# A second attention written out in a fixed order on three engines, with its PSUM banks in three groups

## The chip, the cores and the metric

The kernel runs on one core of one Trainium2 chip. The metric is the device time of one execution in microseconds (us). Before the change the median of 3 runs is 1372.56 us (1369.76 to 1373.3). One further execution was profiled, and everything said of single instructions comes from it.

## The reference, cut to what matters

A batch of 32 sequences of 128 tokens, each token 128 wide, goes through two layers. Each has an attention part and a feed-forward part, both with residual additions, all in fp32.

```python
x = x + L0_attn(L0_cond(x, cond))     # modulated linear layer, 16 heads of 64, causal
x = x + L0_ffn(L0_cond2(x, cond))     # gated recurrence, then three coupling cycles
x = x + L1_attn(L1_cond(x, cond))     # experts, then 16 heads of 8
x = x + L1_ffn(L1_cond2(x, cond))     # low-rank adapter, then a slot memory
```

The change lies in the second layer. Its parts are, shortened:

```python
def L1_cond(x, c):                    # 2 of 4 experts per sequence, and a shared one
    out = sum_e(w[b, e] * mask[e] * (gelu(x @ ew1[e] + eb1[e]) @ ew2[e] + eb2[e]))
    return out + gelu(x @ sw1 + sb1) @ sw2 + sb2

def L1_attn(x, Wq, bq, Wk, bk, Wv, bv, gamma, beta):      # H = 16, dh = 8
    Q, K, V = relu(x @ Wq + bq), relu(x @ Wk + bk), relu(x @ Wv + bv)
    scores = einsum('bqhd,bkhd->bhqk', Qh, Kh) / sqrt(dh)
    scores = where(key_mask == 0 or above the diagonal, NEG, scores)
    out = einsum('bhqk,bkhd->bqhd', softmax(scores) * query_mask, Vh)
    out = out + x
    return gamma * (out - mean(out)) / sqrt(var(out) + 1e-8) + beta

def L1_ffn(x):                        # 64 slots
    alpha = softmax over the 8 best of 64 of (gelu([x, mean(slots)] @ w1 + b1) @ w2 + b2)
    S = GRU(slots, alpha.T @ x / sum(alpha));  S = layernorm(S + selfattention(S))
    return (alpha @ (S @ wvp + bvp)) @ wo + bo
```

## The kernel before, in words

The activations stay in SBUF as `X`, transposed: 128 features on the partitions, 4096 tokens along the free axis. Work goes by chunks of 4 sequences (512 tokens, `CB`, `CH`), 8 chunks in all. The first layer takes the first half of the time and the second layer the rest.

Instructions are written in Python in program order; a scheduler of the framework then orders them on each engine by its own estimate of when their inputs are there, and gives each tile a buffer. Where a call goes through `keep_in_program_order`, the instruction may not be moved ahead of what was written just before it on its engine. Before the change only ACT's activations are held so (`act`, line 337). TensorE and DVE are free. Every PSUM tile is one bank (128 x 512 fp32) and comes from one pool of 8 (`ps`, line 264).

The second layer runs in 4 turns of 32 steps (loop from line 1247), two chunks a turn, here called a and c.

- Steps 0 to 23 are the experts, `experts` (788): per chunk four pieces for the shared expert and eight for the chosen ones. A chosen piece gathers its weights with an indirect DMA issued by POOL (`ew`), makes four hidden blocks on TensorE, four Gelu activations on ACT (`he`), four accumulating matmuls, and two DVE operations that add the result to `xm`.
- `attention_inputs` (827) makes queries, keys, values, mask and residual of a chunk, with six PSUM banks: for a at step 13, for c at step 24.
- Steps 24 to 31 are the attention. A unit is one sequence (`attention`, 865), eight units a turn. Its 16 heads are four groups of four; a group fills one PSUM bank. A unit takes five calls of `advance` (1229), so that five units are under way: `scores` (POOL makes the head-masked keys `km`; four mask matmuls and four score matmuls into four banks), `weights` (per group a DVE maximum, `s1max`, and four exponentials on ACT, `s`), `turned` (per group four transposes, then a copy to SBUF `p1T` on DVE or ACT), `values` (16 small matmuls, a copy `oS` on ACT) and `normed` (four transposes, the division by the sums on DVE, the residual addition on POOL, and the statistics `bn_stats`, `bn_aggr` on DVE).
- After the eighth unit one more `advance` stands in step 31, and three stand in steps 0, 1 and 2 of the next turn, after the expert piece of that step. They drain the last units.
- The rest of a turn's work is generators that take one step an iteration, set by `plan` (1207 to 1226): `after_attention` (953), `hidden`, `routes_top`, `routes` during the next turn's experts, `slots_new` (1057) from its steps 22 and 23, and `slots_told` (1113) from its steps 29 and 30, beside the next turn's attention. After the last turn they run alone.

ACT swaps its function table (`ACT_TABLE_LOAD`) between the Gelu of the experts and the exponential of the attention. `shared` (793) is the first piece of a turn: a matmul from `X`, a Gelu `hid`, a second matmul.

## Time and profile before

| what | value |
| --- | --- |
| median of 3 runs | 1372.56 us (1369.76 to 1373.3) |
| the profiled execution, its own time | 1377.57 us |
| its span, first to last instruction | 1375.8 us |
| mean granted TensorE clock in it | 0.932 |
| busy: TensorE, ACT, DVE, POOL | 1190.6, 782.6, 759.2, 495.4 us |
| weight loads of TensorE (beside the matmuls) | 721.4 us |
| maxima of the second attention on DVE (L888) | 128, first at 770.6, last at 1282.4 us |
| exponentials of the second attention on ACT (L339, `s`) | 512, mean 399 ns |

Busy time is an average over stages. What the change can move lies between 760 and 1300 us, where turns of experts and attention alternate; the first maxima of the four turns stand at 770.6, 913.0, 1070.6 and 1231.2 us. Idle time in front of an instruction is put down in the profile to what released it. "Granted clock" is the share of full speed that TensorE was given in a stretch. In a row of the timeline the instructions of one kind that follow each other are merged, and the time is from the first start to the last end; a row can begin before the one above it has ended, since matmuls overlap, so lengths are best taken from start to start.

### The profile page before, as it was taken

What the parts mean: (1) busy time and instruction counts of PE and PEld (TensorE: products, weight loads), DVE (VectorE), ACT (ScalarE), POOL (GpSimd) and SP (SyncE); (2) the same over time, 40 slices, a digit from 0 to 9 for tenths busy, and PEclk for the clock granted to TensorE, in tenths of its full rate; (3) what the DMA queues carried; (4) which work ended last, traced back from release to release, by engine and by line L of the source; (5) the groups of instructions that cost most, each with busy time, mean ns of one, the idle gap of its engine ahead of it and who ended that gap; (6) DMA issues with size and microseconds to landing.
All of it is one profiled execution on the core that took longest, in us unless ns stands there. A gap on an engine that the chain in (4) does not pass through costs nothing. (4 is left out here: it accounts for less than half of the span.)

```text
span 1375.8 us, 20779 instructions
## 1 busy us (share of the span) xinstructions
PE 1190.6 (87%) x7711; PEld 721.4 (52%) x7711; DVE 759.2 (55%) x1870; ACT 782.6 (57%) x2055; POOL 495.4 (36%) x444
## 2 busy tenths in 40 slices
PE   4999898979898998977787889898899989998865
PEld 1565554535554455534444556655567456665633
DVE  1445665565857558573433764466543665456744
ACT  2765565556657465642355774568545684658522
POOL 1655655465555555552544311221023110311100
PEclk9999999989999899978899999999999899999876
DMA  6000000000000000000242202320044001310000
GB/s 242 1 1 1 1 1 0 1 1 0 1 1 1 0 1 1 1 1 0 95 130 70 70 1 85 107 87 2 8 147 137 2 1 51 121 36 1 9 8 16
DMA packets 15988, 49.67 MB, mean 36 GB/s; under 512 B 1424, under 2 KB 5648, under 8 KB 15504
## 3 DMA queue, kind: packets, MB, share of 16 engines
q0 software_dynamic: 9504, 40.01, 9.3%
q1 hardware_dynamic: 5808, 7.29, 1.5%
q8 instruction: 61, 1.00, 0.3%
q10 hardware_dynamic: 576, 1.05, 0.2%
q14 instruction: 39, 0.32, 0.1%
HBM read 46.25 MB, written 2.10 MB: 35 GB/s over the span
## 5 line engine op out<-in xcount | busy, mean ns | idle before, releaser
L339 ACT ACTIVATE s_sb<-ps,s_max 128x128 f32<-128x128 f32 x512 | 139.0, 382 | 138.4 <-DVE s_max L426 134.8
L279 POOL TENSOR_TENSOR s_sb<-s_sb,s_sum 128x1024 f32<-128x1024 f32 x64 | 121.5, 1898 | 64.7 <-DVE s_sum L435 48.8
L339 ACT ACTIVATE s<-ps,s1max 128x128 f32<-128x128 f32 x512 | 138.1, 399 | 8.0 <-DVE s1max L888 8.0
L268 PE MATMUL ps<-hT,w_attn 128*128 128x512 f32 x256 | 126.2, 624 | 11.4 <-DVE hT L279 11.4
L279 POOL TENSOR_TENSOR s_half<-s_sb 128x512 f32<-128x512 f32 x64 | 82.5, 1289 | 117.1 <-ACT s_sb L339 116.9
L812 POOL DMA_INDIRECT ew<-in_expert,rows x64 | 62.6, 978 | 136.6 <-DVE ye L822 131.5
L339 ACT ACT_TABLE_LOAD x62 | 79.5, 1283 | 53.3 <-DVE s_max L426 38.9
L339 ACT ACTIVATE he<-ps,ew 128x128 f32<-128x128 f32 x256 | 72.6, 369 | 65.3 <-issue 31.2
L888 DVE TENSOR_REDUCE s1max<-ps 128x4 f32<-128x512 f32 x128 | 81.1, 682 | 50.5 <-PE ps L268 42.5
L339 ACT ACTIVATE qk<-ps 128x512 f32<-128x512 f32 x128 | 74.4, 615 | 59.6 <-PE ps L268 59.2
L426 DVE TENSOR_REDUCE s_max<-ps 128x4 f32<-128x512 f32 x128 | 81.0, 674 | 46.3 <-PE ps L268 46.2
L434 DVE TENSOR_REDUCE s_sum<-s_half 128x8 f32<-128x256 f32 x64 | 26.6, 416 | 132.6 <-POOL s_half L279 132.6
L268 PE MATMUL ps<-he,ew 128*128 128x128 f32 x512 | 82.2, 302 | 12.1 <-ACT he L339 11.2
L268 PEld LDWEIGHTS ps<-he,ew 128*128 128x128 f32 x512 | 72.3, 205 | 30.1 <-ACT he L339 27.4
L268 PEld LDWEIGHTS ps<-hT,w_attn 128*128 128x128 f32 x256 | 47.8, 196 | 69.7 <-issue 48.2
L279 POOL TENSOR_TENSOR km<-kT,w_base 128x512 f32<-128x512 f32 x32 | 34.4, 1074 | 132.9 <-PE ps L268 103.4
L268 PEld LDWEIGHTS ps<-qk 64*128 64x128 f32 x1024 | 65.1, 195 | 32.3 <-issue 32.3
L822 DVE SCALAR_TENSOR_TENSOR ye<-ps,ew 128x128 f32<-128x128 f32 x64 | 22.4, 350 | 105.6 <-PE ps L268 105.6
L898 PE MATMUL ps<-w_base,s 128*128 128x128 f32 x512 | 71.1, 287 | 9.8 <-DVE p1T L902 4.6
L268 PE MATMUL ps<-qk 64*128 64x128 f32 x1024 | 77.9, 294 | 0.0
L268 PE MATMUL ps<-pT,v 128*64 128x128 f32 x1024 | 72.4, 285 | 6.1 <-ACT pT L339 5.7
L444 PE MATMUL ps<-w_base,s_sb 128*128 128x128 f32 x512 | 73.9, 289 | 3.6 <-DVE oT L456 3.6
(300 smaller groups left out, 2480.2 us busy)
## 6 DMA issues: line engine op xcount, KB each, us to landing
w_attn<-in_attn POOLq DMA_DIRECT2D x2, 1024.0 KB, 10.5
out_x<-ot SPq DMA_DIRECT2D x8, 256.0 KB, 2.3
X<-in_xT ACTq DMA_DIRECT2D x4, 256.0 KB, 7.5
X<-in_xT SPq DMA_DIRECT2D x4, 256.0 KB, 9.3
w_lowr<-in_lowr SPq DMA_DIRECT2D x1, 1024.0 KB, 12.3
ew<-in_expert,rows POOLq DMA_INDIRECT x64, 4.5
w_ffn<-in_ffn SPq DMA_DIRECT2D x1, 928.0 KB, 10.2
w_mix<-in_mix SPq DMA_DIRECT2D x1, 800.0 KB, 11.1
```

The lines of the kernel that those rows point to most:

```text
L268: T.matmul(out_, lhsT=lhsT, rhs=rhs, start=start, stop=stop)
L279: eng.tensor_tensor(out_, a, b, op)
L339: return tc.keep_in_program_order(A.activation(*args, **kwargs))
L426: V.tensor_reduce(nm[:, 4 * par : 4 * par + 4], b3(two[par]), AX.X, ALU.max, negate=True)
L434: V.tensor_reduce(sm, half[:, :, 0:32], AX.X, ALU.add)
L444: T.transpose(p[:, bass.ts(i, S)], at["s"][:, 4 * par + i, :], ident)
L812: G.indirect_dma_start(ew, None, table, bass.IndirectOffsetOnAxis(ap=rows[:, r, k : k + 1], axis=0))
L822: V.scalar_tensor_tensor(t, y, ew[:, 1028:1029], ew[:, 1029:EW], ALU.add, ALU.mult)
L888: V.tensor_reduce(at["nm"][:, bass.ts(hg, 4)], b3(p), AX.X, ALU.max, negate=True)
L898: T.transpose(p[:, bass.ts(j, S)], at["s"][:, 4 * hg + j, :], ident)
```

## The change

Five things change, and no arithmetic is added or removed.

1. TensorE and DVE are wrapped so that, inside `advance`, each of their instructions is held in program order, as ACT's are already.
2. The one PSUM pool of 8 banks becomes three groups: A with 2, B with 3, C with 3. The first layer takes them in the turn A A B B B C C C. In the second layer every tile comes from C, with these exceptions: the experts' hidden blocks take B, their sums take A, and the attention's scores take the five of A and B in turn.
3. `attention` is cut into nine steps, and `advance` writes them out in one interleaving: the mask matmuls of the next unit are spread over the unit, one as each of the five banks comes free, and the copies out of PSUM are apart from what fills the bank.
4. The first unit's `advance` moves from step 24 to step 23, after the last expert piece, ahead of `attention_inputs` of chunk c. The other calls of `advance` move to the head of their iteration, ahead of its expert piece and generators.
5. `bn_stats` and `bn_aggr` move from `normed` to `after_attention`, and the `f_w1a` matmuls of both chunks are issued together for the odd one.

```diff
-    V, G, A, T = nc.vector, nc.gpsimd, nc.scalar, nc.tensor
+    pinned = []
+    class Pinned:
...
+            def call(*args, **kwargs):
+                ins = f(*args, **kwargs)
+                return tc.keep_in_program_order(ins) if pinned else ins
...
+    V, G, A, T = Pinned(nc.vector), nc.gpsimd, nc.scalar, Pinned(nc.tensor)
...
+    RING = "AABBBCCC"
+    turn = {"all": 0, "scores": 0}
+    short = []
+    def bank(tag):
+        return psum.tile([P, 512], F32, tag="ps" + tag, name="ps", bufs=RING.count(tag))
     def ps():
-        return psum.tile([P, 512], F32, tag="ps", name="ps")
+        if short:
+            return bank("C")
+        turn["all"] += 1
+        return bank(RING[(turn["all"] - 1) % 8])
+    def ps_scores():
+        turn["scores"] += 1
+        return bank(RING[(turn["scores"] - 1) % 5])
...
+        short.append(True)
...
             def shared(k):
-                p = ps()
+                p = bank("B")
...
-                    at["p"] = ps()
+                    at["p"] = bank("A")
...
-                    at["y"] = ps()
+                    at["y"] = bank("A")
...
-                p = ps()
+                p = bank("B")
...
+            def masks(hg):
+                if hg == 0:
+                    at["km"] = pool.tile([P, 4, S], F32, tag="km", name="km")
+                    tt(G, at["km"], outer(kT[:, cs], 4), inner(hmask, S), ALU.mult)
+                    at["p"] = []
+                p = ps_scores()
+                mm(p, ident16, outer(mask16[:, b], 4), stop=False)
+                at["p"].append(p)
...
-                st = pool.tile([P, 6], F32, tag="st", name="st", bufs=2)
-                V.bn_stats(st, Rb)
-                V.bn_aggr(MVs[g][:, b, :], st)
...
+            for b in range(CB):
+                st = pool.tile([P, 6], F32, tag="st", name="st", bufs=2)
+                V.bn_stats(st, R[:, b, :])
+                V.bn_aggr(mv[:, b, :], st)
...
-            if g % 2 == 0:
+            if g % 2:
                 HSs[g // 2] = ps()
-            e = slice(g % 2 * NS, g % 2 * NS + NS)
-            mm(HSs[g // 2][e], w("f_w1a"), xc)
+                for k in range(2):
+                    mm(HSs[g // 2][NS * k : NS * k + NS], w("f_w1a"), XCs[g - 1 + k])
...
-            for hg in range(4):
-                if w1:
-                    w1[1](hg)
-                if t1:
-                    t1[2](hg)
-            if v1:
-                v1[3]()
-            if item:
-                item[0]()
-            if n1:
-                n1[4]()
+            pinned.append(True)
+            do(item, "masks", 0)
+            do(w1, "highest", 0)
+            do(w1, "highest", 1)
+            do(t1, "turned", 0)
+            do(w1, "weights", 0)
+            do(t1, "kept", 0)
+            do(t1, "turned", 1)
+            do(t1, "turned", 2)
+            do(w1, "highest", 2)
+            do(t1, "kept", 1)
+            do(w1, "weights", 1)
+            do(t1, "kept", 2)
+            do(item, "masks", 1)
+            do(t1, "turned", 3)
+            do(w1, "highest", 3)
+            do(v1, "values")
+            do(item, "masks", 2)
+            do(w1, "weights", 2)
+            do(item, "masks", 3)
+            do(v1, "valued")
+            do(item, "scores")
+            do(w1, "weights", 3)
+            do(t1, "kept", 3)
+            do(n1, "normed")
+            pinned.pop()
...
+            if k < 3 and 1 <= r <= NP:
+                advance()
+            if k >= 24 and r < NP:
+                b = k - 23
+                advance(attention(2 * r + b // CB, b % CB) if b < 2 * CB else None)
+                if k == 24:
+                    attention_inputs(2 * r + 1)
             if k == 0 and r < NP:
                 pieces = experts(2 * r) + experts(2 * r + 1)
             if k < 24 and r < NP:
                 pieces[k]()
-            if k == 24 and r < NP:
-                attention_inputs(2 * r + 1)
-            if k < 3 and 1 <= r <= NP:
-                advance()
...
-            if k >= 24 and r < NP:
-                b = k - 24
-                advance(attention(2 * r + b // CB, b % CB))
-                if k == TURN - 1:
-                    advance()
+            if k == 23 and r < NP:
+                advance(attention(2 * r, 0))
```

More of the change, by code (lines that the diff above doesn't have):

```diff
@@ L241, in program, with __init__, __getattr__ @@
     nc = tc.nc
-    V, G, A, T = nc.vector, nc.gpsimd, nc.scalar, nc.tensor
+    pinned = []
+    class Pinned:
+        def __init__(self, engine):
+            self.engine = engine
+        def __getattr__(self, name):
+            f = getattr(self.engine, name)
+            def call(*args, **kwargs):
+                ins = f(*args, **kwargs)
+                return tc.keep_in_program_order(ins) if pinned else ins
+            return call
+    V, G, A, T = Pinned(nc.vector), nc.gpsimd, nc.scalar, Pinned(nc.tensor)
     wpool = ctx.enter_context(tc.tile_pool(name="weights", bufs=1))
-    psum = ctx.enter_context(tc.tile_pool(name="psum", bufs=8, space=bass.MemoryType.PSUM))
+    psum = ctx.enter_context(tc.tile_pool(name="psum", bufs=1, space=bass.MemoryType.PSUM))
     small = ctx.enter_context(tc.tile_pool(name="small", bufs=1))
@@ L869, in attention @@
             at = {}
-            def scores():
-                km = pool.tile([P, 4, S], F32, tag="km", name="km")
-                tt(G, km, outer(kT[:, cs], 4), inner(hmask, S), ALU.mult)
-                four = [ps() for _ in range(4)]
-                for hg in range(4):
-                    mm(four[hg], ident16, outer(mask16[:, b], 4), stop=False)
+            def masks(hg):
[6 more added lines that the diff above has]
+                at["p"].append(p)
@@ L878, in scores, with highest @@
+            def scores():
                 for hg in range(4):
                     r = slice(32 * hg, 32 * hg + 32)
-                    mm(four[hg], qT[r, cs], km[r].rearrange("p j s -> p (j s)"), start=False)
-                at["p"] = four
+                    mm(at["p"][hg], qT[r, cs], at["km"][r].rearrange("p j s -> p (j s)"), start=False)
+            def highest(hg):
+                if hg == 0:
+                    at["nm"] = pool.tile([P, 16], F32, tag="s1max", name="s1max", bufs=2)
+                V.tensor_reduce(at["nm"][:, bass.ts(hg, 4)], b3(at["p"][hg]), AX.X, ALU.max, negate=True)
@@ L883, in weights @@
             def weights(hg):
-                p = at["p"][hg]
                 if hg == 0:
                     at["s"] = pool.tile([P, 16, S], F32, tag="s1", name="s1", bufs=2)
-                    at["nm"] = pool.tile([P, 16], F32, tag="s1max", name="s1max", bufs=2)
-                V.tensor_reduce(at["nm"][:, bass.ts(hg, 4)], b3(p), AX.X, ALU.max, negate=True)
                 for j in range(4):
                     h = 4 * hg + j
-                    act(at["s"][:, h, :], p[:, bass.ts(j, S)], AF.Exp, bias=at["nm"][:, h : h + 1])
+                    act(at["s"][:, h, :], at["p"][hg][:, bass.ts(j, S)], AF.Exp, bias=at["nm"][:, h : h + 1])
@@ L893, in turned, with kept @@
             def turned(hg):
+                p = at["t", hg] = ps()
+                for j in range(4):
+                    T.transpose(p[:, bass.ts(j, S)], at["s"][:, 4 * hg + j, :], ident)
+            def kept(hg):
                 if hg == 0:
                     at["pT"] = pool.tile([P, 16, S], F32, tag="p1T", name="p1T", bufs=2)
-                p = ps()
-                for j in range(4):
-                    T.transpose(p[:, bass.ts(j, S)], at["s"][:, 4 * hg + j, :], ident)
+                p = at["t", hg]
@@ L904, in values @@
             def values():
-                p = ps()
+                p = at["v"] = ps()
                 for hg in range(4):
@@ L910, in values, with valued @@
                         mm(p[32 * j : 32 * j + 32, bass.ts(hg, S)], V1[g % 2 * CB + b][:, h, :], at["pT"][:, h, :])
+            def valued():
                 oS = mpool.tile([P, 4, S], F32, tag="th", name="oS")
-                act(oS, b3(p), AF.Copy)
+                act(oS, b3(at["v"]), AF.Copy)
                 at["o"] = oS
@@ L926, in normed @@
                 tt(G, Rb, Rb, o.rearrange("p h d -> p (h d)"), ALU.add)
-                st = pool.tile([P, 6], F32, tag="st", name="st", bufs=2)
-                V.bn_stats(st, Rb)
-                V.bn_aggr(MVs[g][:, b, :], st)
-            return scores, weights, turned, values, normed
+            return dict(
+                masks=masks, scores=scores, highest=highest, weights=weights, turned=turned, kept=kept,
+                values=values, valued=valued, normed=normed,
+            )
         def root_of(var, name, eps):
@@ L1233, in advance, with do @@
             w1, t1, v1, n1 = (line[-k] if k <= len(line) else None for k in (2, 3, 4, 5))
-            for hg in range(4):
-                if w1:
-                    w1[1](hg)
-                if t1:
-                    t1[2](hg)
-            if v1:
-                v1[3]()
-            if item:
-                item[0]()
-            if n1:
-                n1[4]()
+            def do(it, name, *args):
+                if it:
+                    it[name](*args)
+            pinned.append(True)
[24 more added lines that the diff above has]
+            pinned.pop()
         running = []
```

## The prediction

> **What bounds the kernel now.** I read the page first: shares by engine, the granted clock by slice, then the groups of the second attention.
>
> ```profile
> PE 1190.6 (87%) x7711; PEld 721.4 (52%) x7711; DVE 759.2 (55%) x1870; ACT 782.6 (57%) x2055; POOL 495.4 (36%) x444
> PEclk9999999989999899978899999999999899999876
> L339 ACT ACTIVATE s<-ps,s1max 128x128 f32<-128x128 f32 x512 | 138.1, 399 | 8.0 <-DVE s1max L888 8.0
> L888 DVE TENSOR_REDUCE s1max<-ps 128x4 f32<-128x512 f32 x128 | 81.1, 682 | 50.5 <-PE ps L268 42.5
> ```
>
> TensorE is nearly always busy, so a gain can only come from its gaps and from stretches at a lower clock. Next I asked for busy time by stretch over turn 3, cut where the attention starts, where the clock changes, where the last exponentials end (1130) and where the experts run freely.
>
> ```profile
> 1063.00:1072.43 9.43, 7.49 (x41) 3.84 (x39) 6.89 (x14) 4.17 (x11) 2.96 (x3) 1.00 0.22 65
> 1072.43:1086.08 13.65, 13.65 (x45) 5.84 (x44) 6.98 (x14) 7.65 (x24) 1.04 (x1) 0.50 0.00 0
> 1086.08:1130.00 43.92, 38.83 (x415) 24.09 (x413) 29.92 (x76) 39.58 (x137) 7.02 (x9) 1.00 0.01 1
> ```
>
> Columns are length, then busy time (and count) of PE, PEld, DVE, ACT and POOL, then the granted clock. For 13.65 us TensorE had half its clock. From 1086 on TensorE and ACT are busy for 88% and 90%: two engines, both nearly full, that wait for each other in turn. The timeline of TensorE shows where.
>
> ```profile
> 1067.78 1.14 PE L268 MATMUL ps<-km,qT 32*128 32x512 f32 x8
> 1070.86 0.59 PE L268 MATMUL ps<-sn,w_ffn 128*32 128x256 f32 x2 [1.94 <-DVE sn L1081]
> ...
> 1101.67 0.66 PE L918 MATMUL ps<-w_base,oS 128*128 128x128 f32 x4
> 1102.16 2.23 PE L898 MATMUL ps<-w_base,s 128*128 128x128 f32 x16
> 1104.77 1.08 PE L268 MATMUL ps<-p1T,v 128*32 128x128 f32 x32 [0.38 <-ACT s L339]
> 1105.78 1.04 PE L268 MATMUL ps<-mask,ident 128*128 128x512 bf16 x4
> 1106.75 1.14 PE L268 MATMUL ps<-km,qT 32*128 32x512 f32 x8
> 1107.82 0.66 PE L918 MATMUL ps<-w_base,oS 128*128 128x128 f32 x4
> ...
> 1131.98 1.12 PE L268 MATMUL ps<-hid,w_moe 128*128 128x512 f32 x2 [2.99 <-ACT hid L339]
> ```
>
> Three places: the start (1.94 us, then the half clock), the steady units (one unit from 1101.67 to 1107.82), and the experts' restart (2.99 us, as the Gelu waits behind the last exponentials and a table load). The list of TensorE's waits in the four attention stretches (770 to 832, 911 to 982, 1068 to 1147, 1229 to 1291) sums to 8.2, 9.5, 9.7 and 6.7 us: 34 us that can be won at most, beside the clock.
>
> **The change, part by part.** No work is added or removed; everything lies in where engines wait.
>
> *A steady unit.* TensorE's own work, from start to start in the rows above: 0.49 (transposes of `oS`), 1.97 (16 transposes; the row of 2.23 holds 0.26 of waiting, other units show 1.97), 1.01, 0.97 and 1.07, so 5.51. ACT's: 16 exponentials at 0.25 apart and three copies at 0.48, so 5.44. The unit took 6.15; turn 1 took 25.5 us for the four from 786.6 to 812.1, 6.38 each. Before, all four maxima come first on DVE, and the next unit's masks and scores stand behind all values and transposes. In the new order, from the first exponential of a unit at 0: groups 0, 1 and 2 and one copy end at 3.5, their bank is free 0.14 later (an exponential lasts 0.39 and is issued every 0.25), the fourth mask ends at 3.9, scores at 5.0, the maximum (0.69) at 5.7, and the next unit's first exponential starts at 5.8. A second loop, through group C, is as long: the last copy of a unit frees (0.60) the bank in which the second transposes of the next go, and these (twice 0.49, 0.2 of drain) feed the second copy: again 5.8. So 5.8, not 5.5. Turn 1: 0.58 x 7 = 4. In turns 2 to 4 the slot memory's steps lie between: five distances from 1089.0 to 1123.5 are 6.9 each, of which TensorE waited 0.7 (0.46, 0.38, 1.54, 0.74 and twice 0.26). Its work of 6.2 and the loop's 0.3 leave 6.5: 0.4 x 8 = 3.3 a turn, 10 in three. Together **14 us**. Bounds: all waits inside the units gone, 24; or none, 0.
>
> [...]
>
> *The start.* The first unit's scores go ahead of `attention_inputs` of chunk c (1062.92 to 1066.82, 3.9 us), and its exponentials (first at 1075.15 now) can start some 10 us earlier. That alone wins nothing where TensorE is full. While 16 exponentials run (4.0 us), TensorE has four masks and about half of the inputs, 2.9 us, so it waits about 1.2; after that the input evacuations (`qT`, `kT`, values, `R`) stand on ACT behind these exponentials, and the next transposes need their banks: 1 more. Against 1.94 and two waits of 0.4: **0**. Between -1.1 a turn (3 us waited) and +1.9. POOL's queue is passed too: `km` of this unit already stands before the last eight gathers of expert weights (it ran at 1030.9), and stays there.
>
> *The restart.* Three times 3.0 us. In the new order 16 transposes, values and `oS` (2.0, 1.0 and 0.5) stand before the matmul that waits for `hid`, so the wait is covered; but `hid` and its table load (1.28) now follow copies of the drain on ACT. What is late next is the second piece. **7 us** of 9; bounds 9 and -4 (another 1.4 at each of three, as the second `hid` costs at 1145).
>
> *The clock.* Stretches at half clock in or just behind the attention last 6.83, 3.41, 3.41, 13.65, 6.83 and 3.41 us; half of their sum, 18.8 us, is lost. The row first: at 1072.43 half clock follows a gap of 1.94 us and little work before it; the same gap at 911 is followed by none and at 1229 by 3.41. [...] by the row closing gaps pays. [...] Here 1086 to 1130 has waits of 0.4 to 1.5 and a clock of 1.00, so I side with the row and take a third, **6 us**; bounds 18.8 and -27.
>
> *The rest.* `bn_stats` and `bn_aggr` (32 x 0.29 and 0.18) move behind the units; DVE is busy 30 of 44 us there, and TensorE's work covers them. In the last turn nothing does: three of four pairs, 1.4 us, unless they run early, which their inputs allow. `f_w1a` (two matmul passes, 0.9 us) waits for the odd chunk, uncovered only at the end. **-1 us** in all. In the first layer the banks rotate in a fixed turn of eight in place of a free pool: 0, between +2 and -3, as only few instructions change place.
>
> Sum: 14 + 0 + 7 + 6 - 1 = 26. The profiled execution took 1377.57 us (span 1375.8, 1.8 around it), 0.4% over the median of the runs; 1377.57 - 26 = 1351.6, and carried to the median, 1372.56 - 26 = **1346.5 us**, 1.9% less.
>
> **The rivals.**
>
> *More: the attention becomes dense and the clock stays up* (0.15). ACT runs ahead by 10 us at the start, and most waits (34) go, with half of the clock's loss (9): 43, so 1329. For it: both engines' sums fit into 5.5. Against: the two loops of 5.8.
>
> *Less: only the steady units win* (0.12). The evacuations queued behind exponentials take back the restart, and the clock stays: 14 - 1, so 1359.5.
>
> *No change* (0.06): what TensorE no longer waits for in the units it waits for at the start, with three masks behind 16 exponentials: 1370.
>
> *Slower: group C* (0.12). TensorE runs in order, so a fill that waits for its bank holds everything behind it, the next masks and scores too. Each turn has 6 fills for `attention_inputs` of c and, from turn 2, 10 of the slot memory among the units: 6 x 4 + 10 x 3 = 54. If each waits for an evacuation behind one group of four exponentials (1.0 us), 54 are lost against 26: 1400. It decides from 0.48 us a fill. For it: eight shared banks become three for these. Against: in the built order most fills stand a whole step behind the evacuation that frees their bank.
>
> **How the numbers follow.** Likeliest case 0.55, its own range 1337 to 1357 (steady units 10 to 18, restart 4 to 9, clock 2 to 10). Two executions of this kernel differ by about 0.3%, 4 us, which is what a measurement can tell from no change. Faster: 0.55 + 0.15 + 0.12 = 0.82; same 0.06; slower 0.12. The range from 1330 to 1376 leaves out half of the case at 1329 and nearly all of the slower one, 0.18.
>
> **What the profile after would show.** Steady distances of the first maxima near 5.8 us in turn 1 and 6.5 later; no wait of 3.0 us for `hid` at the restart; the first exponentials of a turn some 5 us after the last expert piece; TensorE's waits in the attention stretches down from 34 us to about 15; half-clock time in them below 30 us. The prediction is wrong if transposes or slot matmuls wait for ACT's evacuations by 0.5 us and more each, if the unit stays above 6.2 in turn 1, or if new half-clock stretches follow the starts.

## The result and the profile after

The changed kernel takes 1349.65 us (median of 4 runs, 1348.0 to 1350.31) against 1372.27 us (1369.76 to 1373.3) of the kernel before: ratio 0.9836, 95% interval 0.9819 to 0.9853, 22.6 us less. The forecast was 26 less, 1346.5. The total came out nearly as said; the way to it did not, so that the agreement is largely luck.

The page of the changed kernel, the lines that answer to those of before (TensorE's and DVE's calls now go through one wrapper, so they all carry line 254; ACT's helper is now line 373):

```profile
PE 1174.8 (87%) x7711; PEld 717.2 (53%) x7711; DVE 752.0 (56%) x1870; ACT 783.2 (58%) x2055; POOL 495.6 (37%) x444
PEclk9999999999989799897899999998999999999866
L373 ACT ACTIVATE s<-ps,s1max 128x128 f32<-128x128 f32 x512 | 143.6, 406 | 50.1 <-DVE s1max L254 50.1
L254 DVE TENSOR_REDUCE s1max<-ps 128x4 f32<-128x512 f32 x128 | 83.7, 679 | 26.4 <-PE ps L254 26.4
```

Before, the exponentials waited 8.0 us for maxima and the maxima 42.5 us for scores. Now the exponentials wait 50.1 us for maxima, and the maxima only 26.4 for scores: DVE, busy for 56%, has become late. That isn't what a faster unit looks like, so the next question is where the 27 us of the profiled spans (1375.8 to 1348.5) went.

I cut the second layer at two kinds of instruction that both kernels have: the last expert addition of a turn (`ye`) and the last copy of values (`oS`). From `ye` to `oS` is an attention stretch; from `oS` to the next `ye` is an expert stretch. First the busy time by stretch of the four attention stretches, of before and then of after (length, then busy time and count of PE, PEld, DVE, ACT and POOL, then granted clock, DMA share and GB/s):

```profile
763.99:832.01 68.02, 58.66 (x555) 35.44 (x556) 46.01 (x159) 52.66 (x166) 12.91 (x16) 0.95 0.07 22
904.53:981.34 76.81, 66.73 (x609) 39.80 (x607) 50.94 (x136) 56.84 (x177) 12.48 (x15) 0.98 0.03 9
1062.17:1142.06 79.89, 70.88 (x609) 40.92 (x607) 51.12 (x137) 57.09 (x177) 12.48 (x15) 0.91 0.03 10
1222.73:1291.65 68.92, 61.87 (x599) 37.39 (x597) 47.84 (x121) 53.96 (x174) 11.51 (x14) 0.98 0.01 1
```

```profile
761.00:834.63 73.63, 57.81 (x554) 34.77 (x554) 46.99 (x159) 50.94 (x164) 12.90 (x16) 0.95 0.07 25
898.49:977.47 78.98, 68.18 (x609) 40.40 (x607) 48.98 (x144) 56.94 (x177) 12.31 (x15) 0.94 0.03 9
1046.43:1124.13 77.70, 66.91 (x609) 40.04 (x607) 48.99 (x145) 57.03 (x177) 12.31 (x15) 0.96 0.03 9
1193.10:1266.62 73.52, 62.04 (x601) 37.86 (x599) 47.13 (x130) 54.93 (x174) 11.29 (x14) 0.98 0.01 1
```

The attention, which the change is about, got longer: 293.6 to 303.8 us. Then the same view of the three expert stretches between, before and after:

```profile
832.01:904.53 72.52, 67.09 (x391) 50.45 (x390) 31.47 (x111) 39.39 (x103) 21.00 (x23) 0.95 0.40 123
981.34:1062.17 80.83, 73.45 (x427) 55.45 (x427) 35.99 (x135) 41.59 (x106) 20.94 (x23) 0.94 0.39 116
1142.06:1222.73 80.67, 73.40 (x427) 55.02 (x427) 35.93 (x135) 41.49 (x107) 17.18 (x19) 0.94 0.29 88
```

```profile
834.63:898.49 63.86, 62.75 (x391) 47.88 (x390) 31.14 (x111) 39.48 (x103) 21.42 (x23) 1.00 0.45 140
977.47:1046.43 68.96, 67.82 (x426) 52.16 (x426) 34.81 (x127) 41.47 (x107) 21.29 (x23) 1.00 0.44 137
1124.13:1193.10 68.97, 67.83 (x426) 52.17 (x426) 34.82 (x127) 41.47 (x107) 17.52 (x19) 1.00 0.34 103
```

These fell from 234.0 to 201.8 us. TensorE stands still for 1.1 us of each (length less PE), where it stood still for 5.4, 7.4 and 7.3, and the clock never drops. So the account of the two profiled spans is: all that comes before the attention -3.0, attention +10.2, expert stretches -32.2, end after the last `oS` -2.2; together -27.2.

Why the expert stretches had waits, and lost them, is to be read from the order of TensorE's rows. The timeline of TensorE just before a turn's chunk c begins with its shared expert, before and after:

```profile
1019.83 1.10 PE L268 MATMUL ps<-w_ffn,hs 64*128 64x64 f32 x8 [1.29 <-ACT hs L339]
1020.86 1.74 PE L268 MATMUL ps<-X,w_moe 128*128 128x512 f32 x2
```

```profile
1009.88 1.88 PE L254 MATMUL ps<-X,w_moe 128*128 128x512 f32 x4
1011.69 1.60 PE L254 MATMUL ps<-w_ffn,hs 64*128 64x64 f32 x16
```

Before, the shared expert's first product (`X,w_moe`) stands behind a small matmul that waits 1.29 us for a Gelu (`hs`). After, two such products are issued first and cover that wait. `one_pool` below, which is the changed kernel with the banks of before, has the old order and the same wait at this place, so it is the banks that let the scheduler put the products first:

```profile
1015.90 1.10 PE L254 MATMUL ps<-w_ffn,hs 64*128 64x64 f32 x8 [1.29 <-ACT hs L373]
```

### The profile page after: what moved, and what is told of

Same layout as the page of the kernel before. It is cut to its first block, busy times and chain, and to the rows that moved or that the text cites. A ratio compares the mean times of both kernels' runs of the same rounds, so it can differ in the third digit from the quotient of the medians.

```text
span 1348.5 us, 20727 instructions
## 1 busy us (share of the span) xinstructions
PE 1174.8 (87%) x7711; PEld 717.2 (53%) x7711; DVE 752.0 (56%) x1870; ACT 783.2 (58%) x2055; POOL 495.6 (37%) x444
## 3 DMA queue, kind: packets, MB, share of 16 engines
q10 hardware_dynamic: 576, 1.05, 0.2%
## 4 chain that ended last, share of the span: by engine, by line
PE 57%; DVE 18%; ACT 15%; POOL 4%; issue 3%; DMA 3%; ACTq 0%; DVEq 0%; POOLq 0%
PE ps L254 57%; ACT s L373 5%; DVE rec L254 4%; ACT s_sb L373 4%; DVE s1max L254 2%; ACT L373 2%; DVE F L254 2%; DVE s_max L254 2%; DVE th L254 1%; DMA ew<-in_expert,rows 1%; POOL s_half L313 1%; POOL v L313 1%; DMA w_ffn<-in_ffn 1%; ACT p1T L373 1%; DMA X<-in_xT 1%
## 5 line engine op out<-in xcount | busy, mean ns | idle before, releaser
L373 ACT ACTIVATE s<-ps,s1max 128x128 f32<-128x128 f32 x512 | 143.6, 406 | 50.1 <-DVE s1max L254 50.1
L254 DVE TENSOR_REDUCE s1max<-ps 128x4 f32<-128x512 f32 x128 | 83.7, 679 | 26.4 <-PE ps L254 26.4
L254 PEld LDWEIGHTS ps<-qk 64*128 64x128 f32 x1024 | 68.9, 196 | 42.4 <-issue 42.4
L254 PE MATMUL ps<-w_base,s_sb 128*128 128x128 f32 x512 | 76.8, 297 | 7.8 <-ACT s_sb L373 6.9
L254 PE MATMUL ps<-qk 64*128 64x128 f32 x1024 | 82.8, 296 | 0.0
L254 PE MATMUL ps<-w_base,s 128*128 128x128 f32 x512 | 72.3, 279 | 11.6 <-DVE o L254 8.4
L254 PEld LDWEIGHTS ps<-w_base,s 128*128 128x128 f32 x512 | 59.4, 142 | 41.8 <-DVE p1T L254 20.7
L254 PE MATMUL ps<-he,ew 128*128 128x128 f32 x512 | 74.7, 290 | 7.1 <-ACT he L373 4.1
L254 PE MATMUL ps<-X,ew 128*128 128x128 f32 x512 | 72.0, 282 | 7.1 <-DMA ew<-in_expert,rows 7.1
L254 PEld LDWEIGHTS ps<-X,ew 128*128 128x128 f32 x512 | 66.7, 197 | 20.4 <-issue 11.4
```

The source lines that it names most:

```text
L254: ins = f(*args, **kwargs)
L373: return tc.keep_in_program_order(A.activation(*args, **kwargs))
```

## The experiments

Ratios are against the kernel before, run on the same chip in the same job. Two executions of one kernel mostly differ by some 0.3%, in some of these kernels by 1%, and the median of the kernel before lay between 1370.2 and 1375.6 in the four jobs of the experiments, so the ratios are what is compared. "A" and "E" are the summed attention and expert stretches of the one profiled execution (that of `one_pool` is the fastest of its five, 6 us below the median).

| kernel | median us | ratio (95% interval) | A | E |
| --- | --- | --- | --- | --- |
| before | 1372.27 | 1 | 293.6 | 234.0 |
| the change | 1349.65 | 0.9836 (0.9819 to 0.9853) | 303.8 | 201.8 |
| groups_only | 1379.78 | 1.0060 (1.0039 to 1.0081) | 325.7 | 206.7 |
| groups_places | 1353.31 | 0.9885 (0.9837 to 0.9932) | 297.3 | 208.6 |
| one_pool | 1360.88 | 0.9918 (0.9887 to 0.9949) | 280.9 | 232.4 |
| old_places | 1361.82 | 0.9934 (0.9912 to 0.9956) | 311.8 | 207.3 |
| free_order | 1342.87 | 0.9799 (0.9764 to 0.9835) | 291.7 | 203.7 |
| pin_pe | 1352.06 | 0.9844 (0.9811 to 0.9877) | 303.7 | 203.5 |
| pin_dve | 1366.92 | 0.9964 (0.9943 to 0.9985) | 314.7 | 202.8 |
| normed_later | 1333.58 | 0.9714 (0.9684 to 0.9744) | 289.8 | 201.8 |
| normed_mid | 1332.38 | 0.9689 (0.9662 to 0.9715) | 287.7 | 202.1 |
| stats_back | 1364.76 | 0.9934 (0.9910 to 0.9959) | 309.5 | 205.5 |
| free_later | 1340.58 | 0.9761 (0.9718 to 0.9804) | 291.7 | 203.7 |
| two_groups | 1337.81 | 0.9743 (0.9717 to 0.9770) | 285.3 | 216.3 |

### The bank groups alone, and everything but the groups

`groups_only` is the kernel before with the three groups and the rings, nothing else:

```diff
-        return psum.tile([P, 512], F32, tag="ps", name="ps")
+        if short:
+            return bank("C")
+        turn["all"] += 1
+        return bank(RING[(turn["all"] - 1) % 8])
...
             def shared(k):
-                p = ps()
+                p = bank("B")
...
-                    at["p"] = ps()
+                    at["p"] = bank("A")
...
-                    at["y"] = ps()
+                    at["y"] = bank("A")
...
-                p = ps()
+                p = bank("B")
...
-                four = [ps() for _ in range(4)]
+                four = [ps_scores() for _ in range(4)]
```

> The kernel before, with nothing but the three bank groups. In the profile after, the attention stretches did not become shorter (last expert product to last copy of oS: 78.4 us in turn 3 against 80.6), but the expert stretches did (last oS to last expert product: 68.3 against 79.9). Theory banks: experts with banks of their own no longer stand behind fills that wait for slow evacuations; then this kernel takes 1354 to 1362 us and its expert stretches of turns 2 and 3 are near 68 to 72 us. Theory order: what shortens them is the order of the instructions; then it takes 1368 to 1385 us, since three banks for all the rest can only hinder, and the expert stretches stay at 78 to 82 us.

`one_pool` is the changed kernel with one pool of 8 for every tile:

```diff
-        return psum.tile([P, 512], F32, tag="ps" + tag, name="ps", bufs=RING.count(tag))
+        return psum.tile([P, 512], F32, tag="ps", name="ps", bufs=8)
```

> The changed kernel with one pool of eight banks, all else as changed. Theory banks: the gain of the expert stretches is lost, 1360 to 1368 us. Theory order: 1346 to 1353 us, expert stretches stay near 68 us.

The groups shorten the expert stretches by 27 us in the old sequence (234.0 to 206.7) and by 31 in the new one (232.4 to 201.8). No kernel with three groups has more than 209, and both with one pool have 232 or more. In the attention they cost about as much: 32 us in the old sequence, 23 in the new one (280.9 to 303.8). The 31 and the 23 are each too large by some 8 us: `one_pool` runs ten records of the shared expert's products (`X,w_moe`) and a few transposes behind the last `oS` of a turn that the changed kernel runs ahead of it, and this work only changes sides. What is left of the 31 is 13 us of TensorE's waits and 9 of clock; what is left of the 23 is 5 of waits and 10 of clock. So the groups alone are slower than nothing (1.0060), the rest of the change without them is worth 0.8%, and the groups on top of it another 0.8%. `groups_only` has the short stretches of "theory banks" (64.1, 71.3 and 71.3 us) and the time of "theory order": neither foresaw so large a cost in the attention. The row of `one_pool` that goes with the second expert stretch above, between the same two instructions, has waits (5.4 us of length less PE) and a clock below 1.00 again:

```profile
979.02:1056.84 77.82, 72.42 (x431) 53.99 (x430) 35.57 (x132) 42.09 (x108) 20.97 (x23) 0.98 0.40 121
```

### The places in the turn, in both sequences

`old_places` is the changed kernel with the loop of before:

```diff
-            if k < 3 and 1 <= r <= NP:
-                advance()
-            if k >= 24 and r < NP:
-                b = k - 23
-                advance(attention(2 * r + b // CB, b % CB) if b < 2 * CB else None)
-                if k == 24:
-                    attention_inputs(2 * r + 1)
...
+            if k == 24 and r < NP:
+                attention_inputs(2 * r + 1)
+            if k < 3 and 1 <= r <= NP:
+                advance()
...
-            if k == 23 and r < NP:
-                advance(attention(2 * r, 0))
+            if k >= 24 and r < NP:
+                b = k - 24
+                advance(attention(2 * r + b // CB, b % CB))
+                if k == TURN - 1:
+                    advance()
```

> The changed kernel with the calls of the attention's steps at their old places: the first unit at step 24 after the inputs of chunk c, the others at the end of their iteration, the three draining ones after the expert piece. Fixed order and bank groups stay. Theory banks and theory order in the units: 1349 to 1355 us, with at most 5 us for the later start. If the places are what helps (the drain written ahead of the expert pieces, so that no Gelu stands ahead of its copies), 1360 to 1372 us and a wait of about 3 us for hid at each restart.

`groups_places` is `groups_only` with the new loop: the old five steps of a unit, no fixed order.

```diff
+            if k < 3 and 1 <= r <= NP:
+                advance()
+            if k >= 24 and r < NP:
+                b = k - 23
+                advance(attention(2 * r + b // CB, b % CB) if b < 2 * CB else None)
+                if k == 24:
+                    attention_inputs(2 * r + 1)
...
-            if k == 24 and r < NP:
-                attention_inputs(2 * r + 1)
-            if k < 3 and 1 <= r <= NP:
-                advance()
...
-            if k >= 24 and r < NP:
-                b = k - 24
-                advance(attention(2 * r + b // CB, b % CB))
-                if k == TURN - 1:
-                    advance()
+            if k == 23 and r < NP:
+                advance(attention(2 * r, 0))
```

> The kernel before with the three bank groups and with the new places of `advance` and `attention_inputs` in the turn; the old five steps of a unit in their old sequence, no fixed order on TensorE and DVE, statistics and `f_w1a` as before. The groups alone gave 1379.8 and the places were worth 12 us in the changed kernel. If the interleaved sequence with masks spread over the unit is what pays for the small groups in the attention, this stays near 1379.8 - 12 = 1368, 25 us above the free kernel with the new sequence; if groups and places are all, it comes to 1343 to 1348.

With the old places TensorE's waits for `hid` come back, 14.6 us in nine waits from the first attention to the last, against one of 2.6 in the changed kernel. The places are worth 1.0% (about 13 us) in the changed kernel and 1.75% (24 us) with the groups and the old sequence. `groups_places` lies between the two expectations. It is 0.9% above the free kernel with the new sequence, which leaves 12 us for the nine interleaved steps and the moved statistics together; how much belongs to either in a free order was not run.

### The fixed order: none, on one engine, on both

`free_order` is the changed kernel in which the wrapper holds nothing:

```diff
-                return tc.keep_in_program_order(ins) if pinned else ins
+                return ins
```

> The changed kernel, but TensorE and DVE are left to the scheduler inside the attention too; bank groups, places and the written sequence stay. Theory banks: 1345 to 1353 us, or less, as the attention's units lose their waits for the first maximum. Theory order: 1362 to 1372 us. If the fixed order of DVE costs what the profile after suggests (the first maximum of a unit starts 1.7 us after its scores end, as the division of an earlier unit stands ahead), the attention stretches get shorter than 76 us in either case.

`pin_pe` and then `pin_dve` wrap one engine only:

```diff
-    V, G, A, T = Pinned(nc.vector), nc.gpsimd, nc.scalar, Pinned(nc.tensor)
+    V, G, A, T = nc.vector, nc.gpsimd, nc.scalar, Pinned(nc.tensor)
```

```diff
-    V, G, A, T = Pinned(nc.vector), nc.gpsimd, nc.scalar, Pinned(nc.tensor)
+    V, G, A, T = Pinned(nc.vector), nc.gpsimd, nc.scalar, nc.tensor
```

> The changed kernel with only TensorE (and ACT, as always) held in program order inside `advance`; DVE is free. The free order of both engines was 1342.9, the fixed order of both 1349.7. If it is DVE's fixed order that costs the 7 us, this gives the free kernel's 1341 to 1345; if it is TensorE's, 1348 to 1352.

> The changed kernel with only DVE (and ACT, as always) held in program order inside `advance`; TensorE is free. If DVE's fixed order costs the 7 us between the free and the fixed kernel, this stays at 1348 to 1352; if TensorE's does, 1341 to 1345. If each costs half, both kernels of this pair stand near 1346.

Without a fixed order the kernel is no slower: 0.9799 against 0.9836, and as the intervals just overlap, the 0.4% between them is not clear of noise. TensorE's order alone gives what both give. DVE's order alone is by far the worst, 0.9964, outside all that was expected: the two don't add. The groups of `free_order` on its page say what happens to the two engines:

```profile
L373 ACT ACTIVATE s<-ps,s1max 128x128 f32<-128x128 f32 x512 | 142.0, 400 | 7.4 <-DVE s1max L254 7.4
L254 DVE TENSOR_REDUCE s1max<-ps 128x4 f32<-128x512 f32 x128 | 83.9, 685 | 66.2 <-PE ps L254 65.6
PE 1209.4 (90%) x7711; PEld 725.8 (54%) x7711; DVE 752.7 (56%) x1870; ACT 782.2 (58%) x2055; POOL 495.2 (37%) x444
```

The 50 us of ACT's waiting for maxima is gone (7.4), the maxima wait for scores again (65.6), and TensorE, with the same 7711 matmuls, is busy for 1209.4 us in place of 1174.8. Where these 35 us come from shows in its timeline, here of one unit of `free_order`:

```profile
1082.27 1.12 PE L254 MATMUL ps<-km,qT 32*128 32x512 f32 x2
1083.32 1.09 PE L254 MATMUL ps<-w_base,s 128*128 128x128 f32 x8
...
1085.89 1.13 PE L254 MATMUL ps<-km,qT 32*128 32x512 f32 x6
1086.96 0.65 PE L254 MATMUL ps<-w_base,oS 128*128 128x128 f32 x4
```

and of one unit of the changed kernel:

```profile
1105.62 1.14 PE L254 MATMUL ps<-km,qT 32*128 32x512 f32 x8
1106.69 0.66 PE L254 MATMUL ps<-w_base,oS 128*128 128x128 f32 x4
```

A unit's scores are four matmuls over 32 rows each, two records apiece, each on another quarter of the 128 rows. Two records alone take 1.05 us from start to start of the next, six take 1.07, and all eight take 1.07: the four run beside each other when they stand together, and one that is cut off costs as much as four. Two records over all 128 rows take 0.9 (`X,w_moe` above, 1.81 for four from 1009.88), so a quarter of the rows saved no time here. Counted over the 32 units, the scores stand in 38 batches before, in 57 in `groups_only` and `groups_places`, in 75 in `free_order`, 87 in `pin_dve`, and in 32 (never cut) in every kernel that fixes TensorE's order. In the free order a score matmul is issued behind its own mask, and with a ring of five banks the masks come one by one. So `free_order` pays 43 x 1.05 = 45 us of TensorE's time for its 43 extra batches (the page shows 35 of them; TensorE counts as busy at half clock too, 13.65 of 13.65 us from 1072.43 before, and over the whole span lost clock is 5 us less in `free_order`, so that 40 are accounted for), and the fixed kernel pays about as much by waiting: TensorE's gaps in the attention sum to 49 us in the changed kernel and 8 in `free_order`. `pin_dve` has 55 extra batches, 12 more than `free_order` (13 us), and in the attention 6 us more of gaps and 3 more of lost clock, together about the 23 us by which its attention is longer. Of the 32 us that `groups_only` lost in the attention, 19 extra batches against before (20 us) and 17 us more of lost clock are more than the whole.

`pin_pe` shows that a free DVE is no cure either. Two lines of its page:

```profile
L373 ACT ACTIVATE s<-ps,s1max 128x128 f32<-128x128 f32 x512 | 141.2, 397 | 10.5 <-DVE s1max L924 10.5
L254 PE MATMUL ps<-w_base,s 128*128 128x128 f32 x512 | 73.0, 280 | 38.6 <-DVE p1T L945 22.9
```

The scheduler puts a unit's four maxima right behind its scores, mostly in a row, and the exponentials wait for them by only 10.5 us. But then the copies `p1T` stand behind 2.5 us of maxima, and the transposes, whose next bank a copy frees, wait 22.9 us for them (38.6 in all, 11.6 in the changed kernel). The attention is as long as with both orders fixed (303.7 and 303.8). So what costs is not that DVE's order is fixed, but what stands in it ahead of an instruction that another engine waits for.

### What makes DVE late: the division, and the statistics

In the changed kernel the timeline of DVE shows what stands in front of a unit's first maximum in turn 3. The scores of these units start on TensorE at 1082.20, 1089.92, 1099.01 and 1105.62:

```profile
1083.96 0.26 DVE L254 RECIPROCAL rsum<-ps 128x16 f32<-128x16 f32 x1 [2.87 <-PE ps L254]
...
1085.09 1.28 DVE L254 TENSOR_REDUCE s1max<-ps 128x4 f32<-128x512 f32 x2
...
1091.81 0.48 DVE L254 TENSOR_REDUCE sl_max<-sl_s 128x2 f32<-128x128 f32 x2 [3.05 <-ACT sl_s L373]
...
1092.81 0.25 DVE L254 RECIPROCAL rsum<-ps 128x16 f32<-128x16 f32 x1
...
1093.57 1.28 DVE L254 TENSOR_REDUCE s1max<-ps 128x4 f32<-128x512 f32 x2
...
1100.59 1.29 DVE L254 TENSOR_REDUCE s1max<-ps 128x4 f32<-128x512 f32 x2 [3.36 <-PE ps L254]
1101.80 0.24 DVE L254 RECIPROCAL rsum<-ps 128x16 f32<-128x16 f32 x1
...
1106.84 1.29 DVE L254 TENSOR_REDUCE s1max<-ps 128x4 f32<-128x512 f32 x2 [1.74 <-PE ps L254]
```

At 1083.96 DVE divides for the unit four before (`normed`), after 2.87 us of waiting for transposes that stand behind this unit's scores on TensorE; only then come the maxima, 1.8 us after the scores were there (1083.3). At 1091.81 a step of the slot memory stands in front as well. In the last two units the division comes after the maxima: an instruction is held only behind the one written just before it on its engine, and I read it so that, where a generator wrote one between that isn't held itself, the two are not tied (not tested by a run). This gives a comparison inside one trace: the distances that end at these first maxima are 7.7 and 8.5 us where the division is ahead, and 7.0 and 6.2 where it is behind.

The longest distances of turns 2 to 4, 12.3 us to the third unit and 10.3 to 11.8 to the fourth, have another cause. There a step of the slot memory stands in front, which waits for TensorE itself:

```profile
1065.22 0.68 DVE L254 TENSOR_TENSOR svs<-ps,w_ffn 64x512 f32<-64x512 f32 x1 [3.49 <-PE ps L254]
...
1067.08 1.28 DVE L254 TENSOR_REDUCE s1max<-ps 128x4 f32<-128x512 f32 x2
```

The scores of this unit were there at 1063.6, so its maximum is 3.5 us late. In turn 1 steps of the routing stand there in the same way (`r_gl`, at 798.71 after 2.89 us of waiting for ACT). The two kernels that follow move only the division, and keep the 12.3 us.

`normed_later` leaves the transposes in place and writes the DVE part behind the first two maxima of the next unit, `normed_mid` behind the first one:

```diff
-            def normed():
-                p = ps()
+            def back():
+                p = at["b"] = ps()
                 for hg in range(4):
                     T.transpose(p[:, bass.ts(hg, P)], at["o"][:, hg, :], ident)
+
+            def normed():
+                p = at["b"]
...
+            done = line[-6] if 6 <= len(line) else None
...
             do(w1, "highest", 0)
             do(w1, "highest", 1)
+            if done and "o2" not in done:
+                done["normed"]()
...
-            do(n1, "normed")
+            do(n1, "back")
+            if n1 and not w1:
+                n1["normed"]()
+                n1["o2"] = True
```

> The changed kernel with `normed` cut in two: its four transposes stay at the end of `advance` (a step `back`), its DVE part (reciprocal, product) is written in the next `advance`, behind the first two maxima (where no unit has maxima due, at once). If DVE's fixed order costs time because it puts the division of an old unit, which waits for transposes, ahead of the next unit's first maximum (the maximum starts 1.7 us after the scores' end in turn 3), some 28 units gain about 0.5 to 1 us each: 1325 to 1338 us. If the units are limited by TensorE's order and the banks, it stays within 4 us of the changed kernel, 1346 to 1353.

```diff
             do(w1, "highest", 0)
-            do(w1, "highest", 1)
             if done and "o2" not in done:
                 done["normed"]()
+            do(w1, "highest", 1)
```

> The kernel with the late division, but behind the first maximum of the next unit in place of behind the second. In the late kernel the second transposes wait for the division to free their bank of group C (1.60, 0.61 and 0.34 us in turn 3, 17.1 us in all with other waits on `o`), and the first group's exponentials cover a second maximum that comes 0.8 us later. If that bank is the limit left: 8 to 16 of the 28 units gain 0.6, so 1324 to 1329. If the second maximum is late instead (the exponentials of a group last 1.0, the maximum would end 1.4 after the first): 0.4 a unit lost, 1340 to 1346.

`normed_later` is 1.2% faster than the changed kernel, 0.9714, where the lateness of DVE was expected to bring it. In the profiled executions the attention fell from 303.8 to 289.8 us: 5.1 of it waiting on TensorE, 8.6 the clock, since half speed cost 13.7 us in the changed kernel and 5.1 here. `normed_mid` shows, on DVE, the order that was wanted: the maximum first, then the slot memory's step and the division.

```profile
1080.59 0.69 DVE L254 TENSOR_REDUCE s1max<-ps 128x4 f32<-128x512 f32 x1 [1.62 <-PE ps L254]
1081.24 0.48 DVE L254 TENSOR_REDUCE sl_max<-sl_s 128x2 f32<-128x128 f32 x2
...
1082.25 0.25 DVE L254 RECIPROCAL rsum<-ps 128x16 f32<-128x16 f32 x1
```

The step from 1333.6 to 1332.4 is within the noise (the intervals overlap), so the bank of group C that the division frees earlier isn't shown to matter by this: TensorE's waits for `o` fell from 17.1 to 9.7 us and the time stayed. The expectation of 1324 to 1329 missed.

`stats_back` goes the other way, and puts the statistics of the unit back behind the division:

```diff
                 tt(G, Rb, Rb, o.rearrange("p h d -> p (h d)"), ALU.add)
+                st = pool.tile([P, 6], F32, tag="st", name="st", bufs=2)
+                V.bn_stats(st, Rb)
+                V.bn_aggr(MVs[g][:, b, :], st)
...
-            for b in range(CB):
-                st = pool.tile([P, 6], F32, tag="st", name="st", bufs=2)
-                V.bn_stats(st, R[:, b, :])
-                V.bn_aggr(mv[:, b, :], st)
```

> The changed kernel with `bn_stats` and `bn_aggr` back at the end of `normed`, held in DVE's order like it. The prediction costed their move at a loss of up to 1.4 us, with DVE free. Held in order, the statistics wait for POOL's addition (0.45 us, and POOL's own queue ahead of it) in front of the next unit's first maximum: if DVE's order ahead of the first maximum sets the pace, 28 units lose 0.5 (statistics) to 1.2 us (with POOL's addition), so 1362 to 1384. If the order on DVE isn't the limit, 1346 to 1351.

It is 1.0% slower than the changed kernel. Its timeline of DVE shows the cost at its worst, the wait for POOL's addition now in front of the maxima:

```profile
1098.35 0.29 DVE L254 TENSOR_TENSOR o<-ps,rsum 128x128 f32<-128x128 f32 x1
1099.21 0.29 DVE L254 BATCH_NORM_STATS2 st<-R 128x6 f32<-128x128 f32 x1 [0.57 <-POOL R L313]
1099.54 0.18 DVE L254 BATCH_NORM_AGGREGATE mv<-st 128x2 f32<-128x6 f32 x1
1099.64 1.26 DVE L254 TENSOR_REDUCE s1max<-ps 128x4 f32<-128x512 f32 x2
```

From `o` to the maximum it is 1.29 us; in the changed kernel it was 0.2. Of the 13.2 us between the two profiled spans 7.1 are clock; the attention has 5.7 of the 13.2, the expert stretches 3.7 and the end 4.6. The sum is what was expected, the place only in part.

`free_later` is the late division without a fixed order (both edits above):

> The kernel with the late division, and TensorE and DVE free (no fixed order). Free order alone took 1342.9 against 1349.7 fixed; the late division took 1333.6 fixed. If a fixed order is worth having once the division stands in the right place, this is slower than 1333.6, near 1340 to 1345 (the scheduler places the division where it likes, so the edit moves little). If the order is a cost in itself and the place of the division was a second fault, both gains add: 1325 to 1330.

It is 1340.6, not told apart from `free_order` (0.9761 against 0.9799, overlapping). So the place of the division matters where the order is fixed. Whether a fixed order is then worth having is not quite shown: like for like, `normed_later` (0.9714) is 0.5% ahead of `free_later` with intervals that overlap. `normed_mid` (0.9689) is clear of it, but has the division one maximum earlier, and that edit was not run without a fixed order.

### Which of the groups

`two_groups` is `normed_mid` with A and B made one:

```diff
     def bank(tag):
+        tag = "C" if tag == "C" else "AB"
-        return psum.tile([P, 512], F32, tag="ps" + tag, name="ps", bufs=RING.count(tag))
+        return psum.tile([P, 512], F32, tag="ps" + tag, name="ps", bufs=5 if tag == "AB" else 3)
```

> The kernel with the division behind the first maximum (1332.4), with groups A and B made one of five banks; C stays apart with three. In all kernels with three groups the four stretches of experts between attentions sum to 202 to 209 us against 232 to 234 with one pool. If what shortens them is that the slot memory and the other small steps (group C) no longer take the experts' banks, this keeps 200 to 204 and 1330 to 1336 us. If the experts' sums, held over four pieces, need banks apart from the hidden blocks too, the stretches go back to 215 and more, and the time to 1345 or above.

The expert stretches sum to 216.3 us, 14 more than in `normed_mid`, as in the second expectation; the time is 0.5% longer and in neither. Of the 14 us, 9 are work that only changes sides, as in `one_pool`, and 5 are TensorE's waits. Counted by these waits, the expert stretches have 16.8 us with one pool (and 8.5 us of lost clock), 8.8 with two groups and 3.4 with three (and next to no lost clock in either). So keeping the small steps (C) apart brings the larger part, and keeping the experts' sums apart from their hidden blocks the smaller one. In the profiled execution all that comes before the attention took 754.3 us against 761.4; a first layer with two groups ahead of a second with three was not run.

## Why the prediction came true, and where it failed

**A steady unit (14 us): failed.** The attention lost 10.2 us, although 6.4 of the waits at the restart went, which lie in it; so the rest of it lost 16.6 where 14 were to be won. The loop was worked out as "scores at 5.0, the maximum (0.69) at 5.7", with nothing between. DVE's fixed order puts the division of an older unit there, which waits for transposes behind the very scores, and beside it the routing's steps in turn 1 and the slot memory's in turns 2 to 4. Steady distances of 5.8 and 6.5 us were forecast; the changed kernel has 9.9, 9.8 and 9.8 for three of the seven in turn 1, and 12.3, 10.4, 7.7, 8.5, 7.0 and 6.2 in turn 3, the last two where the division is behind the maximum. A unit above 6.2 us in turn 1 was named as a sign that the prediction is wrong, and it came. The working had counted TensorE's and ACT's order through the loop, and DVE only by the duration of its maximum. `normed_later` and `stats_back` move the time by 1.2% down and 1.0% up with DVE's order alone, so the cost of what stands there is shown for the division and the statistics. For the slot memory's and the routing's steps it is read from the timeline alone. What the fixed order does win, scores that are never cut (6 extra batches before, 6 us), was not in the sum either.

**The clock (6 us): right in size, and not all of it.** Half speed cost 94.7 us of the whole span before and 81.0 after, counted as half of the time spent at it: before, a batch of scores takes 2.00 and 2.02 us at half clock (from 1074.97 and 1077.51, start to start), where at full clock it is 1.05 and 1.07. Of the stretches that the prediction listed in or just behind the attention (18.8 us), the attention's own cost 13.7 us in both kernels; the two just behind it, from 987.10 and 1147.52, are gone, which is 5.1 us. The other 8.5 us that went lay further inside the expert stretches and had not been listed. The bound of -27 stood for one more stretch of 13.65 us in each turn, half of it lost. It was an estimate, and none of that length came: the longest in the attention of the changed kernel is 6.83 us.

**The restart (7 us): right.** The wait of 3.0 us is gone in turns 2 and 3; turn 1 keeps 2.6 of it. That is 6.4 of 9. The timeline of TensorE in the changed kernel, turns 1 and 3:

```profile
831.76 1.13 PE L254 MATMUL ps<-hid,w_moe 128*128 128x512 f32 x2 [2.60 <-ACT hid L373]
```

```profile
1120.97 0.86 PE L254 MATMUL ps<-p1T,v 128*32 128x128 f32 x22
1121.76 1.13 PE L254 MATMUL ps<-hid,w_moe 128*128 128x512 f32 x2
```

In turn 3 most of a unit's values stand in front of the matmul that waited, and cover it.

**The start (0): no gain, as said, and rather a loss.** The first maximum of turns 2 to 4 stands 2.9 us after the last expert addition (8.5 before). But by the first maximum of the fourth unit TensorE has stood still for 5.0 us a turn, against 2.1 to 3.1 before; the bound was 3. The longest of these waits is that of a mask for exponentials, which wait for the maximum that the slot memory's step holds up.

```profile
1069.05 0.49 PE L254 MATMUL ps<-mask,ident 128*128 128x512 bf16 x1 [2.23 <-ACT s L373]
```

Start, restart and drain together, which is what `old_places` undoes, are worth 1.0%, about 13 us. The sum had 7 for them; `old_places` doesn't tell the three apart.

**The rest (-1): wrong in sign and size.** The move of the statistics was costed by DVE's 0.29 and 0.18 us a unit, as if they only had to be covered. In a fixed order what counts is what they would hold up, and by `stats_back` the move is worth 1.0%, 13 us (5.7 of them in the attention).

**What the sum left out: the expert stretches (32 us).** The bank groups were treated as a cost of the attention (the rival "group C") and never as a gain elsewhere. `one_pool` and `groups_only` show that the gain is theirs, but for some 8 us of work that changes sides in `one_pool`. The waits that they removed stood in the profile of before: in the second expert stretch 1.9, 1.5, 1.4, 1.3 and 1.1 us (`al`, `he`, `hid`, `hs`, `y`), 7.2 in all, and 5.1 us of clock. I had listed TensorE's waits in the four attention stretches only.

**The rivals.** "Only the steady units win" was the opposite of what happened. "Group C" was right in that smaller groups cost: without the 8 us of work that changes sides, they take 15 us in the attention of the new sequence. That is not shown to be C's alone, since TensorE waits there 26.2 us for exponentials, which free the banks of A and B, and 8.4 for the division, which frees those of C. It didn't decide, because the same groups won 22 us outside the attention. TensorE's waits in the attention, forecast to fall from 34 to 15 us, rose to 49. By the stretches, the forecast was -21 for the attention beside the clock, and for the expert stretches no more than their share of the clock's 6; it came to +10 and -32. Two errors of about 30 us and of opposite sign met the forecast of 26, and that they cancel is luck.

`normed_mid`, at 1332.4 us, 1.5% below the changed kernel, is the best version that was run. Two things that the traces suggest were not tried: a first maximum that is held behind nothing, with all the rest fixed, and the first layer's banks taken from two groups.

## What to carry to other kernels

Before you fix an order by hand, write out for every engine, the one with time to spare too, what stands in front of the instruction that the next engine waits for: a fixed order is worth no more than its worst entry, and an engine that is half idle (DVE here, busy for 56%) can set the pace by what stands in front. A pool of banks shared by two stages ties their orders together, so a change of pools is to be costed in every stage that draws from it, not only in the one that is rewritten. And where a free order is compared with a fixed one, compare the engine's busy time for the same number of instructions as well as its waits.

## What the runs showed of the hardware that was not expected

- Four score matmuls over 32 rows each take 1.07 us together and 1.05 us for one alone. A scheduler that issues them as they become ready costs 43 batches, 45 us, in `free_order`.
- Waits of 1.3 to 1.9 us were followed by half clock in the expert stretches of before. After the wait of 1.29 us that ended at 1019.83 the busy time by stretch shows

```profile
1012.50:1021.23 8.73, 7.44 (x60) 7.05 (x59) 2.75 (x7) 6.27 (x13) 4.29 (x4) 1.00 0.57 186
1021.23:1024.64 3.41, 3.41 (x11) 2.38 (x10) 2.76 (x16) 1.68 (x5) 0.15 (x1) 0.50 0.59 177
```

  The wait is in the first row (8.73 long, 7.44 busy), the half clock in the second. All seven half-clock stretches of the expert parts began 0.8 to 2.1 us after such a wait had ended, and with these waits gone (the longest that is left is 1.1 us) there were none.
- The same wait was not followed by the same loss of clock. In the changed kernel a mask waits 2.23 us near the start of turn 2 (until 921.11) and of turn 3 (until 1069.05). The clock is at 0.50 for 6.83 us after the first (922.40 to 929.23) and for 3.41 us after the second (1069.18 to 1072.59). What makes the difference is not shown.
